# Product 7 of each projection in block products, with its shared terms added through an SBUF buffer

## The chip, the cores and the metric

The kernel runs on one core of a Trainium2 chip. The time is what the device takes for one execution of the whole program, in microseconds (us). Before the change it is 1493.05 us, the median of 10 runs that lie between 1492.59 and 1495.52 us.

## The reference

The input is x, 128 images of 128 nodes with 512 features each, and one 128x128 matrix adj with many zeros. Two layers follow each other, and both work on h, the layer norm of their input with negative values set to 0. All numbers are float32. Cut to what matters:

```python
h = jnp.maximum(_layernorm(x, axis=-1), 0.0)
A = jnp.einsum('od,bdn->bon', W1, h)            # W1 = W2 = adj
C = jnp.einsum('od,bdn->bon', W2, h) + b[None, :, None]
pre = A[:, :, None, :] + (C - A)[:, :, :, None]
x = x + jnp.max(jax.nn.relu(pre), axis=-1)      # layer 0

h = jnp.maximum(_layernorm(x, axis=-1), 0.0)    # layer 1
q = (h @ Wq + bq).reshape(b, n, H, HD)          # k and v the same; H, HD = 8, 64
scores = jnp.einsum('bihd,bjhd->bhij', q, k) / jnp.sqrt(jnp.float32(HD))
scores = scores + jnp.where(adj == 0, -1e9, 0.0)
out = jnp.einsum('bhij,bjhd->bihd', jax.nn.softmax(scores, axis=-1), v)
x = x + out.reshape(b, n, H * HD)
```

Layer 0 adds to each row of x one number per node, max(0, max over n of (adj @ h) + b), because A cancels on the diagonal of `pre`. A number that is the same for a whole row doesn't change a layer norm, so layer 1's h is that of layer 0, and the number (C in the kernel) is only added to x.

## The kernel before

The 128 images are worked on in 32 groups of G = 4. One pass of the main loop does, for group g: `apply(g - 1)` (attention weights times v, 128 small matmuls on TensorE, then reciprocals and products on VectorE), `scores(g)` (64 matmuls of q and k, and the exponentials on ScalarE), the projection v of group g, and the projections q and k of group g + 1. The norms of group g + 2, their adjacency products (adj @ h, one 128x512 matmul whose row maximum VectorE takes), the masks (GpSimd multiplies the exponentials by 0 or 1), the bias of v (`add_bv`), the number C (`add_c`, ScalarE) and the residuals of group g - 1 are spread over the pass.

The order in which each engine's instructions stand is written out by hand. Each projection is a list of six parts; v has parts 0 to 5, q 6 to 11, k 12 to 17. The table `todo` names what else is issued behind which part, and every engine works its own list from front to back.

A projection is a product of 512x512 matrices (512 rows of h, 512 outputs). It is computed after Strassen and Winograd: weights and activations are cut in quarters a11 to a22 and b11 to b22; sums s1 to s4 of the weight quarters (`weight_sum`) and t1 to t4 of the activation quarters (`h_sum`) are formed, and seven products of quarters replace eight. Products 1, 6 and 7 are accumulated in one another's terms, so that product 7's result stands in three outputs' sums: two of them take it, one through the term in `u3` (with product 5) and one through the PSUM bank of products 6 and 7, into which product 4 is accumulated afterwards.

Products 1, 6 and 7 are four matmuls each, 128x128 weights by 128x256 (`mm`, L453). Products 2, 3, 4 and 5 are split once more in the same way, into seven matmuls of 128x128 by 128x128 (`block_mm`, L561). The sums for that are `weight_blocks` (once, for the weights) and `h_blocks` (per group, on GpSimd, L380: one operation of 128x256 and two of 128x128 for each product). Three of the seven block products ("inner" ones) go straight into the PSUM bank of the product. The other four are shared by several outputs: they are accumulated in a scratch region (`run`, `five`) and added from there to the SBUF terms by VectorE (`more`, L579), step by step: the first and the fifth, then the sixth, then the seventh. Each next step accumulates into the same region, so it waits until VectorE has read the one before.

The terms lie in `pf` (product 1, with the terms of product 5's blocks) and in `u` (two parts, for the outputs that products 4 and 3 complete); `u` has two buffers. `add_pf` (L496, or L492 for v) adds a PSUM bank, a bias and `pf`. `add` (L474) writes an output as bank plus term. PSUM has eight banks, `bank(0)` to `bank(7)`, and a bank is used anew when its last reader is done.

Layout: h of a group is transposed by VectorE in blocks of 32 (`blocks`) and moved into place, `hT`, by 16 DMAs on SP's queue (`move`); `hT` has two buffers. All sums t1 to t4 and the results of `h_blocks` have one buffer each, so group g + 1's overwrite group g's.

In passes 0 and 31, v is computed with plain products. Product 7 is line `self.mm(self.b, "s3", "t3", ...)` in `p7`.

## Time and profile before

| what | value |
|---|---|
| median of 10 runs | 1493.05 us |
| the profiled execution | 1491.48 us |
| its span, first to last instruction | 1489.6 us |
| granted TensorE clock | 0.998 |
| TensorE busy (matmul) | 1472.1 us |
| VectorE / ScalarE / GpSimd busy | 1183.9 / 595.8 / 978.9 us |
| one pass of the loop (start of `apply` to the next, e.g. 773.65 to 819.32) | 45.67 us |

In the profile PE is TensorE, PEld its weight loads, DVE VectorE, ACT ScalarE, POOL GpSimd, and SP the engine that issues most DMAs. L453 is line 453 of the kernel. A line of a timeline gives the start, the time from the first start to the last end, the engine, the line, the operation, output <- inputs by name, and how often it stands there in a row; in brackets stands idle time before it and what ended it. The records of one TensorE instruction overlap with the next, so distances of starts tell its cost. A matmul of this kernel is two instructions.

### The profile page before, as it was taken

What the parts mean: (1) busy time and instruction counts of PE and PEld (TensorE: products, weight loads), DVE (VectorE), ACT (ScalarE), POOL (GpSimd) and SP (SyncE); (2) the same over time, 40 slices, a digit from 0 to 9 for tenths busy, and PEclk for the clock granted to TensorE, in tenths of its full rate; (3) what the DMA queues carried; (4) which work ended last, traced back from release to release, by engine and by line L of the source; (5) the groups of instructions that cost most, each with busy time, mean ns of one, the idle gap of its engine ahead of it and who ended that gap; (6) DMA issues with size and microseconds to landing.
All of it is one profiled execution on the core that took longest, in us unless ns stands there. A gap on an engine that the chain in (4) does not pass through costs nothing.

```text
span 1489.6 us, 36725 instructions
## 1 busy us (share of the span) xinstructions
PE 1472.1 (99%) x14013; PEld 1328.4 (89%) x14013; DVE 1183.9 (79%) x2869; ACT 595.8 (40%) x1179; POOL 978.9 (66%) x1238
## 2 busy tenths in 40 slices
PE   8999999999999999999999999999999999999997
PEld 6889989899998999898988999999999989899996
DVE  6787878878888878788787887788877878877886
ACT  3334343444344343434434443434434343444332
POOL 5887675667665676756677566766567675667660
PEclk9999999999999999999999999999999999999999
DMA  5221333212332223332123322233221233212211
GB/s 171 51 75 36 77 86 83 68 36 77 82 86 69 67 46 78 86 77 72 37 74 85 87 66 49 63 82 86 70 72 41 77 86 86 65 37 76 68 44 59
DMA packets 307826, 105.55 MB, mean 71 GB/s; under 512 B 273152, under 2 KB 273280, under 8 KB 307648
## 3 DMA queue, kind: packets, MB, share of 16 engines
q1 hardware_dynamic: 307328, 102.84, 27.6%
q8 instruction: 113, 1.85, 0.6%
q14 instruction: 65, 0.53, 0.1%
q0 software_dynamic: 176, 0.27, 0.1%
q10 hardware_dynamic: 144, 0.07, 0.0%
HBM read 37.03 MB, written 33.55 MB: 47 GB/s over the span
## 4 chain that ended last, share of the span: by engine, by line
PE 94%; POOL 2%; DVE 1%; DMA 1%; issue 0%; ACT 0%; SPq 0%; DVEq 0%; POOLq 0%
PE bk L561 39%; PE bk L453 33%; PE bk L720 8%; PE bk L690 8%; PE bk L343 7%; DMA wk_sb<-in_L_gnn_Wk_dram 1%; POOL ssq_sb L401 0%; POOL xp L311 0%; POOL o L750 0%; ACT hn L305 0%; DVE hs L367 0%; POOL rstd L286 0%; POOL h L380 0%; DVE ssk_sb L401 0%; POOL sq_sb L413 0%
## 5 line engine op out<-in xcount | busy, mean ns | idle before, releaser
L702 POOL TENSOR_TENSOR w<-w,live 128x512 f32<-128x512 f32 x248 | 309.2, 1274 | 0.0
L750 POOL TENSOR_TENSOR o<-xp,o 128x512 f32<-128x512 f32 x122 | 152.6, 1283 | 204.8 <-DVE o L738 174.9
L579 DVE TENSOR_TENSOR u<-u,bk 128x256 f32<-128x256 f32 x552 | 204.9, 412 | 57.7 <-PE bk L561 57.7
L698 ACT ACTIVATE w<-bk 128x512 f32<-128x512 f32 x256 | 128.8, 628 | 275.7 <-PE bk L690 275.7
L481 ACT COPY p1a<-bk 128x512 f32<-128x512 f32 x95 | 55.6, 586 | 388.7 <-PE bk L453 379.2
L380 POOL TENSOR_TENSOR h<-hT 128x256 f32<-128x256 f32 x93 | 68.2, 734 | 211.0 <-DMA hT<-tb 85.5
L579 DVE TENSOR_TENSOR p1a<-p1a,bk 128x128 f32<-128x128 f32 x368 | 109.4, 318 | 120.0 <-PE bk L561 62.9
L311 POOL TENSOR_TENSOR xp<-xp,bv_sb 128x512 f32<-128x512 f32 x128 | 160.1, 1271 | 32.3 <-ACT hn L305 32.3
L305 ACT ACTIVATE hn<-xp,nmr,rstd 128x512 f32<-128x512 f32 x124 | 100.9, 814 | 87.8 <-POOL nmr L288 47.9
L453 PE MATMUL bk<-hs,sk_sb 128*128 128x256 f32 x512 | 131.4, 380 | 0.0
L453 PE MATMUL bk<-sv_sb,hs 128*128 128x256 f32 x512 | 131.0, 380 | 0.0
L453 PE MATMUL bk<-hs,sq_sb 128*128 128x256 f32 x496 | 127.9, 380 | 0.0
L343 PE MATMUL bk<-hn,adjT 128*128 128x512 f32 x248 | 126.9, 593 | 0.0
L720 PE MATMUL bk<-v,w 128*64 128x65 f32 x4096 | 126.5, 222 | 0.0
L720 PEld LDWEIGHTS bk<-v,w 128*64 128x64 f32 x4096 | 122.1, 137 | 4.1 <-issue 0.3
L690 PE MATMUL bk<-qT,kT 64*128 64x128 f32 x2048 | 122.9, 275 | 0.0
L690 PEld LDWEIGHTS bk<-qT,kT 64*128 64x128 f32 x2048 | 116.8, 188 | 2.5 <-issue 0.3
L380 POOL TENSOR_TENSOR h<-hT,h 128x128 f32<-128x128 f32 x186 | 108.1, 581 | 14.6
L453 PEld LDWEIGHTS bk<-sv_sb,hs 128*128 128x128 f32 x512 | 90.4, 191 | 21.3 <-issue 14.3
L738 DVE TENSOR_TENSOR o<-bk,RS 128x448 f32<-128x448 f32 (+1 forms) x161 | 93.7, 582 | 7.2
L561 PEld LDWEIGHTS bk<-h,ssk_sb 128*128 128x128 f32 x558 | 81.8, 191 | 16.0 <-issue 14.3
L453 PEld LDWEIGHTS bk<-hs,sk_sb 128*128 128x128 f32 x512 | 87.8, 191 | 7.6 <-issue 0.7
(181 smaller groups left out, 3590.7 us busy)
## 6 DMA issues: line engine op xcount, KB each, us to landing
out_dram<-o SPq DMA_DIRECT2D x128, 256.0 KB, 2.6
xp<-in_x_dram SPq DMA_DIRECT2D x62, 512.0 KB, 4.0
hT<-tb SPq DMA_DIRECT2D x992, 32.0 KB, 1.9
xp<-in_x_dram SPq DMA_DIRECT2D x4, 256.0 KB, 4.3
wq_sb<-in_L_gnn_Wq_dram SPq DMA_DIRECT2D x2, 512.0 KB, 8.6
wk_sb<-in_L_gnn_Wk_dram SPq DMA_DIRECT2D x2, 512.0 KB, 10.9
wv_sb<-in_L_gnn_Wv_dram SPq DMA_DIRECT2D x2, 512.0 KB, 11.8
bv_sb<-in_L_gnn_bv_dram POOLq DMA_DIRECT2D x1, 256.0 KB, 8.0
```

What stands on the lines that cost most here:

```text
L305: nc.scalar.activation(HN[m], x_of(m), AF.Relu, scale=RSTD[m], bias=NMR[m])
L311: nc.gpsimd.tensor_tensor(x_m, x_m, bv_sb, op=ALU.add)
L343: nc.tensor.matmul(pa, adjT, HN[m], start=True, stop=True)
L380: nc.gpsimd.tensor_tensor(o, x, y, op=ALU.subtract)
L453: nc.tensor.matmul(bank[:, r, :], lhs, rhs, start=first and r == 0 and c == 0, stop=r == 1 and c == 1, skip_group_check=True,)
L561: nc.tensor.matmul(out, lhs, rhs, start=start, stop=True, skip_group_check=True)
L579: nc.vector.tensor_tensor(to, to, what, op=ALU.add)
L690: nc.tensor.matmul(psc[j][:, f, :], KT[g][r, f, i * D : (i + 1) * D], QT[g][r, f, i * D : (i + 1) * D], start=True, stop=True,)
L698: nc.scalar.activation(w[:, j], psc[j], AF.Exp, scale=HD ** -0.5)
L702: eng.tensor_tensor(w[:, j], w[:, j], live_h, op=ALU.mult)
L720: nc.tensor.matmul(pav[r, c : c + HE], w[:, h % 2, h // 2, r], V[:, i, h, :], start=True, stop=True,)
L750: eng.tensor_tensor(y, x_of(b), y, op=ALU.add)
```

## The change

Product 7 of q and k of groups 1 to 31, and of v in passes 1 to 30, is split into seven block products too. Its sums: a fifth set of weight blocks (`weight_blocks` of s3; for v in a tile of its own, for q and k in place of a quarter that is not needed) and a fifth `h_blocks` per group, of t3.

Its four shared block products are not added to one term but to two (product 7's result is in two outputs). So they are collected in a new SBUF buffer T7: ScalarE copies the first and the fifth into it, VectorE adds the sixth and the seventh, ScalarE copies the seventh into the one quarter that holds it alone. Then GpSimd adds the whole buffer, 128x512, to the two terms (`terms7(0)`, `terms7(1)`). `pf`, `u` and `u3` become one tile U of three parts with one buffer, and T7 has one buffer.

The order changes with it. The list of parts is now made by `steps`; product 5 of q, k and v has its first blocks ahead of product 6, product 7's first blocks stand between product 6's matmuls, and product 3's output (`end3`) is written in the second part of the next projection. The sums t3 and t4 (`h_sum` 0 and 3) go from VectorE to GpSimd. `h_blocks` is issued in its single operations, in another order. The adjacency product is split into `product` (TensorE) and `maximum` (VectorE). Norms, `blocks`, `move`, `add_bv` and masks are issued at other parts; the heads of `apply` are taken in the order 0, 2, 4, 6, 1, 3, 5, 7. The weight blocks of q and v in pass 0 are issued in other places and partly on VectorE instead of GpSimd.

The core of the diff (`u[:, 0]` is product 1's term and then product 7's, `u[:, 1]` goes to product 4's output, `u[:, 2]` to product 3's):

```diff
+    U = const.tile([P, 3, 2, N // 2], F32, name="u")
+    T7 = const.tile([P, 2, N // 2], F32, name="t7")
...
-        def h_blocks(g, k):
+        def h_blocks(g, k, parts=range(3)):
...
+            sums = (
                 (t[:, 0:2], b[:, :, 1], b[:, 0]),
                 (t[:, 2], b[:, 1, 1], t[:, 0]),
                 (t[:, 3], b[:, 1, 0], t[:, 2]),
-            ):
+            )
+            for i in parts:
+                o, x, y = sums[i]
                 nc.gpsimd.tensor_tensor(o, x, y, op=ALU.subtract)
...
+            def end7(self):
+                self.add_pf(self.u[:, 0], self.b, 1)
...
+            def end5(self):
+                self.add(self.dst(1, 1), self.c, self.u[:, 0])
...
+            def inner(self, k):
+
+                x = self.bk({5: self.c, 3: self.c, 7: self.b, 4: self.b, 2: self.a}[k])
+                a, b, s, t = self.parts_of(k)
+                self.block_mm(x[:, 0, 0], a[:, 0, 1], b[:, 1, 0])
+                self.block_mm(x[:, 0, 1], s[3], b[:, 1, 1])
+                self.block_mm(x[:, 1, 0], a[:, 1, 1], t[:, 3])
...
+            def sixth(self, k):
+                a, b, s, t = self.parts_of(k)
+                self.block_mm(self.run[k], s[2], t[:, 2])
+
+            def seventh(self, k):
+                a, b, s, t = self.parts_of(k)
+                self.block_mm(self.run[k], s[1], t[:, 1])
...
+            def first_to(self, k):
+                if k == 7:
+                    self.t = self.bk(T7)
+                    nc.scalar.copy(self.t[:, 0, 0], self.run[7])
+                    nc.scalar.copy(self.t[:, :, 1], self.five[7].unsqueeze(1).to_broadcast([P, 2, D]))
+                    return
+                self.add_blocks(k, 0, 0, 1)
...
+            def terms7(self, i):
+
+                u = self.u[:, i]
+                nc.gpsimd.tensor_tensor(u, u, T7, op=ALU.add)
+
+            def seventh_to(self, k):
+                if k == 7:
+                    nc.scalar.copy(self.t[:, 1, 0], self.run[7])
+                    self.add_blocks(7, 1, 1, 7)
+                    return
+                self.add_blocks(k, 1, slice(0, 2), 7)
+
+        def steps(p, tail, mid, t3):
+
+            t = tail + [lambda: None] * 8
+            return [
+                [t[0], p.p1],
+                [call(p.first, 5, True), call(p.first_to, 5), t[1], call(p.p6a, (0,)),
+                 call(p.first, 7, True), call(p.first_to, 7), call(p.p6a, (1, 2)),
+                 call(p.sixth, 5), call(p.sixth_to, 5), call(p.sixth, 7), call(p.sixth_to, 7),
+                 call(p.p6a, (3,)), call(p.seventh, 5), call(p.seventh_to, 5), p.end6],
+                [call(p.first, 2, True), call(p.seventh, 7), call(p.seventh_to, 7), call(p.terms7, 0), mid,
+                 call(p.inner, 2), p.end2, call(p.inner, 5), call(p.first43), call(p.first_to, 2),
+                 call(p.first_to, 4),
+                 call(p.inner, 7), t3, call(p.terms7, 1)],
+                [p.end7, p.end5],
+                [call(p.sixth, 2), call(p.sixth_to, 2), call(p.sixth, 4), call(p.sixth, 3), call(p.sixth_to, 4)],
+                [call(p.inner, 4), call(p.inner, 3), call(p.seventh, 2), call(p.seventh, 4),
+                 call(p.seventh, 3), call(p.seventh_to, 2), call(p.seventh_to, 4), p.end4],
+            ]
+
+        def later(p):
+            return [lambda: None, p.end3]
...
-                for h in range(H):
+                for h in (0, 2, 4, 6, 1, 3, 5, 7):
...
-                0: [(norm_end, m, False), (norm_end, m + 1, False)],
-                1: [(blocks, m)], 2: [(blocks, m + 1)],
-                4: [(adjacency, m)], 5: [(move, m + 1)], 7: [(adjacency, m + 1), (norm_act, m + 2)],
-                8: [(norm_end, m + 2), (add_bv, m), (add_bv, m + 1)],
-                13: [(norm_act, m + 3)], 14: [(norm_end, m + 3)], 16: [(adjacency, m + 2)],
+                1: [(norm_end, m, False)], 4: [(norm_end, m + 1, False)],
+                3: [(product, m)], 5: [(maximum, m)],
+                8: [(norm_act, m + 2)],
+                9: [(product, m + 1)], 10: [(blocks, m), (norm_end, m + 2, False), (norm_act, m + 3)], 11: [(blocks, m + 1), (move, m + 1), (maximum, m + 1)],
+                13: [(blocks, m + 2)], 14: [(norm_end, m + 3, False)],
+                15: [(product, m + 2)] + [(add_bv, m + i) for i in range(4)],
+                16: [(maximum, m + 2), (blocks, m + 3), (move, m + 3)],
...
+                    if p.n == "v":
+                        t3 = lambda: h_sum(g + 1, 0, nc.gpsimd)
+                    if p.n == "q":
+                        mid = lambda: [
+                            h_blocks(g + 1, k, (i,)) for k, i in ((0, 1), (1, 1), (0, 2), (1, 2))
+                        ]
...
-                        blocks(m - 2)
-                        blocks(m - 1)
-                        move(m - 1)
                         for i in range(G):
                             residual(b - G + i, nc.gpsimd)
...
+                    for k in (1, 2):
+                        add(4, h_sum, g + 1, k)
+                    for k, i in ((4, 0), (4, 1), (3, 0), (3, 1)):
+                        add(4, h_blocks, g + 1, k, (i,))
+                    add(5, h_sum, g + 1, 3, nc.gpsimd)
+                    for k, i in ((2, 0), (3, 2), (2, 1), (2, 2), (0, 0), (1, 0), (4, 2)):
+                        add(5, h_blocks, g + 1, k, (i,))
...
-                    for k, s in enumerate((8, 9, 9, 10, 10, 13, 14, 15)):
+                    for k, s in enumerate((8, 8, 9, 9, 14, 14, 14, 14)):
                         add(s, mask, nc.gpsimd, b + k // 2, k % 2)
...
-                    add(4, weight_blocks, nc.gpsimd, "v", (3, 2))
-                    add(15, weight_blocks, nc.gpsimd, "v", (0, 1))
+                    for s, k in ((0, 2), (0, 0), (1, 1)):
+                        add(s, weight_blocks, nc.vector, "q", (k,))
+                    for s, k in ((0, 3), (0, 2), (1, 0), (1, 1), (2, 4)):
+                        add(s, weight_blocks, nc.vector if k in (3, 2) else nc.gpsimd, "v", (k,))
+                    add(3, weight_blocks, nc.gpsimd, "q", (4,))
                     for i in range(G):
-                        add(15, add_bv, i)
+                        add((3, 3, 3, 11)[i], add_bv, i)
```

A part's own steps are issued first, then what `todo` names for it. `steps` is given for each projection; `tail` is `later` of the projection before, so its `end3` stands behind the first blocks of product 5.

## The prediction

> **What bounds the kernel now.** I read the page first (busy shares, then the chain that ended last), then one whole pass of the loop in the table by windows, then that pass in order of time, engine by engine.
>
> ```profile
> span 1489.6 us, 36725 instructions
> ...
> PE 1472.1 (99%) x14013; PEld 1328.4 (89%) x14013; DVE 1183.9 (79%) x2869; ACT 595.8 (40%) x1179; POOL 978.9 (66%) x1238
> ...
> PE 94%; POOL 2%; DVE 1%; DMA 1%; issue 0%; ACT 0%; SPq 0%; DVEq 0%; POOLq 0%
> ```
>
> ```profile
> core 0: us, PE busy (x) PEld busy (x) DVE busy (x) ACT busy (x) POOL busy (x), PEclk, DMA share, GB/s
> ...
> 773.65:819.32 45.67, 45.67 (x441) 41.41 (x441) 36.73 (x90) 18.69 (x37) 30.53 (x39) 1.00 0.28 70
> ```
>
> TensorE is the bound: 94% of the chain, no idle time in a pass, at a granted clock of 1.00. A pass (from the first matmul of `apply` to the next one) takes 45.67 us, and the others have room: VectorE 36.7, GpSimd 30.5, ScalarE 18.7 us. So less TensorE work shows in full as long as nobody makes TensorE wait.
>
> What one product costs is read from the starts of TensorE's instructions (two per matmul), not from their durations, which overlap:
>
> ```profile
> 786.39 0.38 PE L561 MATMUL bk<-wv_sb,h 128*128 128x128 f32 x2
> 786.61 0.39 PE L561 MATMUL bk<-wv_sb,hT 128*128 128x128 f32 x2
> ...
> 788.62 1.03 PE L453 MATMUL bk<-sv_sb,hs 128*128 128x256 f32 x4
> 789.49 0.38 PE L561 MATMUL bk<-ssv_sb,h 128*128 128x128 f32 x2
> 789.71 1.03 PE L453 MATMUL bk<-sv_sb,hs 128*128 128x256 f32 x4
> 790.58 0.38 PE L561 MATMUL bk<-sv_sb,hT 128*128 128x128 f32 x2
> ```
>
> Ten 128x128 blocks lie between 786.39 and 788.62: 0.223 us each. Product 7 is the four 128x256 matmuls from 788.62 to 790.58 with one block (789.49 to 789.71) between them: 1.96 - 0.22 = 1.74 us, 0.435 each.
>
> **The change, part by part.**
>
> *Product 7 in blocks.* Seven blocks for four matmuls: 7 x 0.223 = 1.56 against 1.74, a gain of 0.18 us. It applies to v in passes 1 to 30 and to q and k of groups 1 to 31, so 92 times: **-16.5 us**, and a pass of 45.67 - 0.54 = 45.13 us if nobody waits. The products' order around it moves the same matmuls, at no cost of their own.
>
> *GpSimd.* Its prices:
>
> ```profile
> 779.60 4.96 POOL L750 TENSOR_TENSOR o<-xp,o 128x512 f32<-128x512 f32 x4 [5.86 <-DVE o L738]
> ...
> 795.02 0.73 POOL L380 TENSOR_TENSOR h<-hT 128x256 f32<-128x256 f32 x1 [1.50 <-DVE hT L367]
> 795.83 1.32 POOL L380 TENSOR_TENSOR h<-hT,h 128x128 f32<-128x128 f32 x2
> 797.10 0.73 POOL L380 TENSOR_TENSOR h<-hT 128x256 f32<-128x256 f32 x1
> 797.91 1.43 POOL L380 TENSOR_TENSOR h<-hT,h 128x128 f32<-128x128 f32 x2
> 799.31 0.73 POOL L380 TENSOR_TENSOR h<-hs 128x256 f32<-128x256 f32 x1
> 800.11 0.99 POOL L380 TENSOR_TENSOR h<-hs,h 128x128 f32<-128x128 f32 x2
> ...
> 806.90 6.19 POOL L702 TENSOR_TENSOR w<-w,live 128x512 f32<-128x512 f32 x5
> ```
>
> Back to back, a 128x512 operation takes 1.23 us, a 128x256 one 0.73, a 128x128 one 0.46 (0.99 for two). A pass gets six adds of the buffer (`terms7`), two sums moved from VectorE (`h_sum` 0 and 3) and three operations of a fifth `h_blocks`: 8 x 1.23 + 0.73 + 2 x 0.46 = 11.5 us, so about 42 of 45.1. It still fits. What matters is where it is late.
>
> *The chain between v and q.* `h_sum` 0 overwrites a tile that v's product 7 reads until its third `inner` block, 17.2 us into the pass (scores end at 7.66, then v's matmuls at the prices above). From there GpSimd's queue holds, in order, without a pause: `h_sum` 0, `terms7(1)` of v, five first parts and six later parts of `h_blocks`, `h_sum` 3 among them, `terms7(0)` of q, four more later parts, `terms7(1)` of q. VectorE's `sixth_to(4)` of q stands behind that last add, since both add into u[:, 1], and TensorE's `seventh(4)` of q overwrites what `sixth_to(4)` reads; q's last blocks, k and the rest are queued behind it.
> GpSimd: 5 x 1.23 = 6.15; 5 first parts at 0.69, their 0.73 less the 0.04 by which independent neighbours overlap (1.27 lasts, 1.23 apart), = 3.45; 10 later parts, seven that follow something else at 0.41 and three that read the one before at 0.54 (795.83 and 800.11 rows: 0.46 and a gap of 0.08) = 4.49. Sum 14.1.
> To it comes contention: where a sum of two SBUF tiles runs on VectorE, the GpSimd operation that starts during it is stretched:
>
> ```profile
> 795.52 0.78 DVE L367 TENSOR_TENSOR hs<-hT 128x512 f32<-128x512 f32 x1
> ...
> 798.35 0.68 DVE L367 TENSOR_TENSOR hs<-hT,hs 128x512 f32<-128x512 f32 x1
> ```
>
> The pair at 795.83 takes 1.32 for 0.99, that at 797.91 1.43: 0.33 and 0.44 more. `h_sum` 1 and 2 stay on VectorE inside this chain: +0.77. The release of the tile costs 0.25 (the first L380 group of the pass starts that long after TensorE's slot ends), the add of `sixth_to(4)` and its hand-over 0.5 (L579, 0.41). Together 15.6 us.
> TensorE meanwhile has 45 blocks, 8 matmuls of 128x256 and 2 adjacency products (0.86 each): 10.04 + 3.46 + 1.72 = 15.2. So it waits **0.4 us in each of the 30 passes that have this chain, +11.7 us**. Bounds: 0 (no stretch, all parts overlapping: 13.7 + 0.75, earlier than needed) and 1.5 (all parts with gaps, 15.2, and both stretches). I take the middle sum because its rows are these very operations.
> The page "SBUF — State Buffer" of the Trainium skill (section "SBUF: two separate sides") says the pair of ports is an exclusive lock held for a whole instruction. By it the two sums would block 0.7 us each, 1.4 instead of 0.77, the wait 1.0 and the time 1508, an estimate from that page; the rows above show less than a whole instruction, so they decide here.
>
> *The hand-over on v alone.* `sixth_to(4)` of v waits for its `terms7(1)`, then `h_sum` 1 and 2 precede `seventh_to(4)`, which frees the bank that q's first blocks use. 17.45 + 2.5 + 0.35 (add) + 1.5 (the sums) + 0.17 (stretch) + 1.0 (three adds) = 23.0, needed at 22.8. This 0.2 lies inside the same 15.2 us and is not added.
>
> *end7.* From the end of `first43`, VectorE does three adds (0.33 apart, the 789.71 group of L579 is 1.05 for three) and the two halves of `end7` (L496, 0.88): 0.2 + 0.99 + 0.88 = 2.07 us; TensorE has `inner(7)`, an adjacency product and three sixths, 0.67 + 0.86 + 0.67 = 2.2, before it writes that bank. Nothing waits, with 0.1 us to spare; without the `product` there it would be 0.7 us late per product.
>
> *ScalarE and VectorE.* Three copies per product on ScalarE (0.24 by L263's 128x128 copy, up to 0.48 by L468 for the 128x256): +2.9 us a pass, under 22 of 45. VectorE gets 6 x 0.28 and loses 2 x 0.7. Both are covered by TensorE.
>
> *Masks and residuals.* k's `terms7(1)` waits for `first_to(4)`, 42.4 us in; four masks follow and end about 3.1 us into the next `apply`. The new order of heads needs the last one at 2.9 + 0.5 = 3.4. Covered with 0.3. Then come four `add_bv` (4.9), so the residuals start at 8 instead of 5.95, and norms end by 14.8; ScalarE's `norm_end(m)` stands ahead of v's last copy of the buffer, so `terms7(0)` of v starts at 15.5 and is needed by 17.7.
>
> *Moves.* SP issues 16 transfers in 11.2 to 11.4 us. Both moves now follow each other (from 35.7): 35.7 + 22.8 = 58.5, that is 13.4 into the next pass, landed (1.9) at 15.3, read at 17.4. The output stores wait behind them till 13.4; the residuals are only then written. Nothing is late.
>
> *Pass 0.* VectorE gets about 24 more `weight_blocks` operations there. Five groups at about 1.4 us (L401) now precede `end6` of v: from 47.2 to 54.2, +0.7, where TensorE needs it at 53.35: 1.6 us, and 0.9 more at the last product. Pass 1 lost 0.9 to late `add_bv` (46.57 against 45.67), and this goes: **+1.6 us**, between -1 and +4.
>
> Sum: -16.5 + 11.7 + 1.6 = **-3.2 us**. The profiled execution (1491.48 with 1.9 around its span) is 1.57 under the median of the runs; from the median 1493.05 I get 1489.9.
>
> **The rivals.**
> 1. *GpSimd is never late.* For it: the bound of 0; in 15.2 us a stretch of 0.4 decides. Against: both VectorE sums fall into the chain. Time: -16.5 + 1.6, to -16.5 + 6 + 1.6 with 0.2 us of waits: 1478 to 1484.
> 2. *Slower: the add into u[:, 1] on q comes later still.* Same place, `sixth_to(4)` of q behind `terms7(1)`, with gaps at every small operation. It decides from 0.5 us per pass on (16.5 - 1.6 = 14.9 over 30). At 0.9 us it costs 27: 1505; at 1.5, 1523. For it: GpSimd at 42 of 45 us and gaps of 0.08 us shown at dependent pairs. Against: most neighbours are independent.
> 3. *ScalarE holds k back.* `norm_end(m+2)` stands on its queue ahead of k's copies and waits for GpSimd's norms (1.05 us by L298 to L302) after q's last add; two norm passes (1.58) and k's first copies follow: 32.3 + 1.05 + 0.7 + 1.58 + 1.9 = 37.5, while k's `sixth(7)` would be at 37.4 to 37.8. Price 0.15 us per pass, +4.5: 1494.4.
> 4. *No saving on TensorE*, weight loads binding at 128 columns: excluded, 0.223 is measured with its loads.
>
> **How the numbers follow.** Forecast (waits of 0.2 to 0.55 us, 1484 to 1495) 0.34; rival 1, 0.22; rival 2, 0.34; rival 3, 0.10. The line at 0.2%, about 3 us, is what a measurement here tells from no change. Faster: all of rival 1 and 0.24 of the forecast, 0.46. Same: 0.08 of the forecast, 0.06 of rival 3, 0.02 of rival 2, 0.16. Slower: 0.38. Range: from rival 1's 1479 to waits of 1.05 us, 1493 + 31.5 - 14.9 = 1510, which leaves a tenth at each end.
>
> **What would show it.** A pass of 45.5 us with TensorE idle only before q's `seventh(4)`, near 32.4 us into it, and at q's first block; product 7 at 1.56 us; GpSimd near 42 us a pass; no idle in `apply` and none at `inner(4)`. It is wrong if TensorE waits at `inner(4)` for `end7`, or in `apply` for a mask, or if GpSimd's 20 operations take clearly under 14.5 or over 15.5 us.

## The result

The changed kernel takes 1503.29 us (median of 8 runs, 1501.84 to 1504.52) against 1493.23 us for the kernel before (28 runs): a ratio of 1.0067, interval [1.0059, 1.0076]. It is 10 us slower. The forecast was 1489.9 us with "faster" as the likeliest sign, and that sign was wrong. The time lies inside the range (1479 to 1510), but for other reasons than those on which the range's upper half was built.

From the page of the changed kernel (its profiled execution took 1502.45 us): the span, the busy times and the shares of the chain that ended last.

```profile
span 1500.7 us, 38618 instructions
...
PE 1474.8 (98%) x14565; PEld 1336.4 (89%) x14565; DVE 1224.0 (82%) x3016; ACT 653.0 (44%) x1455; POOL 1317.6 (88%) x1564
...
PE 93%; DVE 3%; issue 1%; POOL 1%; DMA 1%; ACT 0%; SPq 0%; DVEq 0%; POOLq 0%
```

TensorE is still the bound, but it is now idle for 25.9 us of the span instead of 17.5, and VectorE's share of the chain went from 1% to 3%. So one looks for places where TensorE waits for VectorE. The table by windows, with one row per pass of the loop, shows two of them (the columns are as in the prediction):

```profile
core 0: us, PE busy (x) PEld busy (x) DVE busy (x) ACT busy (x) POOL busy (x), PEclk, DMA share, GB/s
...
91.34:136.98 45.64, 45.60 (x460) 41.62 (x459) 37.36 (x95) 20.48 (x46) 41.59 (x50) 1.00 0.28 70
182.61:229.15 46.54, 45.85 (x459) 41.53 (x458) 38.57 (x95) 20.61 (x46) 41.60 (x50) 1.00 0.27 70
```

The normal pass of 45.64 us is as long as before (45.67), although product 7 costs less in each of the three projections. And some passes, like the second row, are 0.9 us longer, with VectorE 1.2 us busier. GpSimd is busy for 41.6 us of a pass, as forecast.

Where each microsecond went, from the starts of the first matmul of each `apply`, which mark the ends of the passes:

| stage | before | after | difference | in the prediction's sum |
|---|---|---|---|---|
| up to the first `apply` (the lead-in and pass 0) | 86.87 | 91.34 | +4.47 | +2.5 |
| pass 1 | 46.57 | 45.64 | -0.93 | -1.05 |
| passes 2 to 29, as if all were median ones (45.67, 45.655) | 1278.76 | 1278.34 | -0.42 | -4.2 |
| passes 2 to 29, what the longer ones have above that | 0.84 | 7.79 | +6.95 | 0 |
| pass 30 | 43.24 | 45.64 | +2.40 | -0.15 |
| from the start of pass 31 to the last instruction | 33.32 | 31.95 | -1.37 | 0 |
| span | 1489.6 | 1500.7 | +11.1 | |

(The last column splits the prediction's terms by stage: 0.54 us gained and 0.39 us waited in each pass from 1 to 30, 2.5 us lost in pass 0 and 0.9 us won back in pass 1. The remainder to its -3.2 us is the two products of group 1 in pass 0. Each column is one execution. Two kernels further down that differ only in pass 30 reach the first `apply` at 90.62 and 91.54, so the first row is known to about 1 us.)

**The normal pass.** TensorE's starts show the gain of product 7 at the size that was forecast. The distance between starts is at least 0.110 us for one instruction of a 128x128 block and 0.215 us for one of a 128x256 matmul, in both kernels. A pass before has 168 and 72 of these, a pass after 210 and 48: 42 x 0.110 - 24 x 0.215 = -0.54 us. But the distances above these minima sum to 0.61 us in a pass before and to 1.12 us in a pass after: +0.51 us. In the fastest kernel further down (a pass of 45.31 us) 0.33 us of these are gone, and 0.18 us stay as gaps of 0.03 to 0.06 us. About 0.33 us of the 0.51 lies in one place, at q's first blocks. There TensorE starts its blocks with gaps, as the timelines of TensorE and VectorE show for the pass that began at 91.34:

```profile
113.86 0.43 PE L587 MATMUL bk<-h,wq_sb 128*128 128x128 f32 x2
114.34 0.46 PE L587 MATMUL bk<-hT,sq_sb 128*128 128x128 f32 x2
114.63 0.60 PE L481 MATMUL bk<-hs,sq_sb 128*128 128x256 f32 x2
```

```profile
111.47 0.83 DVE L379 TENSOR_TENSOR hT<-hT 128x512 f32<-128x512 f32 x1
112.34 0.83 DVE L379 TENSOR_TENSOR hs<-hT 128x512 f32<-128x512 f32 x1
113.09 0.41 DVE L639 TENSOR_TENSOR v<-v,bk 128x256 f32<-128x256 f32 x1
113.42 0.74 DVE L665 TENSOR_TENSOR u<-u,bk 128x256 f32<-128x256 f32 x2
```

The block (two instructions) at 113.86 takes 0.48 us from start to start and the next one 0.29, where a block takes 0.22 elsewhere. VectorE's two sums (`h_sum` 1 and 2, L379) stand ahead of v's last adds (L639, L665), which read the bank that q's first blocks overwrite. This is the "hand-over on v alone" of the prediction.

The chain on GpSimd behind it is there too, with the lengths that the prediction worked out. These are its rows from `h_sum` 0 to the middle, and its last add:

```profile
108.57 1.27 POOL L379 TENSOR_TENSOR hs<-hT 128x512 f32<-128x512 f32 x1 [0.67 <-PE bk L587]
...
111.83 0.79 POOL L396 TENSOR_TENSOR h<-hs,h 128x128 f32<-128x128 f32 x1
112.58 1.17 POOL L396 TENSOR_TENSOR h<-hT 128x256 f32<-128x256 f32 x1
...
122.22 1.26 POOL L690 TENSOR_TENSOR u<-u,t 128x512 f32<-128x512 f32 x1
```

From 108.57 to 123.48 are 14.9 us (forecast 14.1 + 0.77), and the two operations that meet VectorE's sums are stretched by 0.33 and 0.44 us over their 0.46 and 0.73. But TensorE doesn't wait for the last add, because it has already lost the time at q's first blocks.

**The long passes.** The timeline of VectorE in a normal pass (first fence) and in a long one (second), about 11 us into the pass:

```profile
147.52 0.69 DVE L352 TENSOR_REDUCE amax<-bk 128x1 f32<-128x512 f32 x1 [2.46 <-PE bk L348]
148.25 0.54 DVE L354 TENSOR_SCALAR c<-amax,b_sb 128x4 f32<-128x4 f32 x1
148.71 0.47 DVE L639 TENSOR_TENSOR u<-u,bk 128x128 f32<-128x128 f32 x2
```

```profile
193.16 0.69 DVE L352 TENSOR_REDUCE amax<-bk 128x1 f32<-128x512 f32 x1 [2.45 <-PE bk L348]
193.88 1.80 DVE L354 TENSOR_SCALAR c<-amax,b_sb 128x4 f32<-128x4 f32 x1
195.59 0.47 DVE L639 TENSOR_TENSOR u<-u,bk 128x128 f32<-128x128 f32 x2
```

The operation at L354 adds a bias to four numbers per partition and clips them: the number C. It took 0.23 us in passes 2 to 29 before. It now takes 0.52 to 0.55 us in 21 of the passes 1 to 29, and 1.80 us in the other 8, which are the long ones. The adds at L639 that free the region for v's sixth block stand behind it on VectorE. TensorE then waits for them:

```profile
195.92 0.49 PE L587 MATMUL bk<-wv_sb,h 128*128 128x128 f32 x2 [0.62 <-DVE u L639]
```

GpSimd runs the four residuals of the group before at that time, back to back (1.23 us apart), in both passes:

```profile
145.03 4.95 POOL L816 TENSOR_TENSOR o<-xp,o 128x512 f32<-128x512 f32 x4
...
190.67 4.95 POOL L816 TENSOR_TENSOR o<-xp,o 128x512 f32<-128x512 f32 x4
```

The short C operation ends at 148.79, just behind the boundary between the third residual and the fourth (145.03 + 3 x 1.23 = 148.7); the long one, which starts the same 0.47 us ahead of that boundary, misses it and ends at 195.68, behind the end of the fourth (195.6). In each of the passes 1 to 29 it ends 0.03 to 0.07 us behind the end of a residual. So this tiny operation waits for a gap between GpSimd's operations, and it sometimes loses the first gap.

The kernel before shows the same effect in its pass 1. There late `add_bv` operations had made the residuals late, and C, which starts 11.72 us into every pass, fell beside the last of them:

```profile
94.75 4.95 POOL L750 TENSOR_TENSOR o<-xp,o 128x512 f32<-128x512 f32 x4
```

```profile
98.59 1.13 DVE L346 TENSOR_SCALAR c<-amax,b_sb 128x4 f32<-128x4 f32 x1
```

It ended at 99.72, behind the residuals' end at 99.70, and TensorE's next block of v came 0.35 us late (99.97). The price of C beside a residual stood in the trace of the kernel before.

**Pass 0.** VectorE's adds stand behind the weight operations that were moved to it. TensorE waits for 2.1 us at 52.3, 1.55 us at 62.3 and 0.9 us at 69.6. The chain of VectorE at the first of these, and TensorE:

```profile
53.34 0.54 DVE L422 TENSOR_TENSOR ssv_sb<-wv_sb,ssv_sb 128x128 f32<-128x128 f32 x1
53.81 0.68 DVE L517 TENSOR_TENSOR u<-bk,u 128x512 f32<-128x512 f32 x1
```

```profile
54.63 2.33 PE L481 MATMUL bk<-sv_sb,hs 128*128 128x256 f32 x5 [1.96 <-DVE u L517]
```

A weight operation like these takes 0.28 us where GpSimd is idle (55.12). Where it is not, most take longer: 0.54 us (53.34) or 1.35 us (58.68).

**Pass 30** has one adjacency product instead of four. Before, it was 2.4 us shorter than the other passes for that reason. Now the 2.6 us of the missing three (0.86 each) are spent on waits instead:

```profile
1440.98 0.71 PE L587 MATMUL bk<-ssv_sb,h 128*128 128x128 f32 x4 [0.28 <-DVE u L665]
...
1453.58 0.68 PE L587 MATMUL bk<-h,ssq_sb 128*128 128x128 f32 x4 [0.38 <-DVE u L665]
```

These are the sixth blocks, which wait for VectorE's three adds of the first ones (L665, 1439.85 to 1440.93).

### The profile page after: what moved, and what is told of

Read it like the earlier page. It is cut to its first block, busy times and chain, and to the rows that moved or that the text cites. A ratio compares the mean times of both kernels' runs of the same rounds, so it can differ in the third digit from the quotient of the medians.

```text
span 1500.7 us, 38618 instructions
## 1 busy us (share of the span) xinstructions
PE 1474.8 (98%) x14565; PEld 1336.4 (89%) x14565; DVE 1224.0 (82%) x3016; ACT 653.0 (44%) x1455; POOL 1317.6 (88%) x1564
## 4 chain that ended last, share of the span: by engine, by line
PE 93%; DVE 3%; issue 1%; POOL 1%; DMA 1%; ACT 0%; SPq 0%; DVEq 0%; POOLq 0%
PE bk L587 48%; PE bk L481 22%; PE bk L786 8%; PE bk L756 8%; PE bk L348 7%; PE bk L732 1%; DMA xp<-in_x_dram 1%; DVE amax L352 0%; DVE ssk_sb L422 0%; POOL w L768 0%; POOL xp L314 0%; POOL o L816 0%; DVE ssq_sb L422 0%; PE bk L340 0%; DVE u L639 0%
## 5 line engine op out<-in xcount | busy, mean ns | idle before, releaser
L690 POOL TENSOR_TENSOR u<-u,t 128x512 f32<-128x512 f32 x184 | 234.3, 1273 | 86.0 <-DVE t L639 62.2
L665 DVE TENSOR_TENSOR u<-u,bk 128x256 f32<-128x256 f32 x552 | 206.6, 415 | 43.8 <-PE bk L587 26.6
L639 DVE TENSOR_TENSOR u<-u,bk 128x128 f32<-128x128 f32 x368 | 109.0, 316 | 79.6 <-PE bk L587 78.7
L352 DVE TENSOR_REDUCE amax<-bk 128x1 f32<-128x512 f32 x128 | 86.7, 677 | 74.7 <-PE bk L348 74.7
L508 ACT COPY u<-bk 128x512 f32<-128x512 f32 x95 | 55.0, 579 | 183.5 <-PE bk L481 175.7
L587 PE MATMUL bk<-ssv_sb,h 128*128 128x128 f32 x720 | 111.6, 277 | 0.3 <-DVE u L665 0.3
L587 PEld LDWEIGHTS bk<-ssv_sb,h 128*128 128x128 f32 x720 | 98.5, 191 | 14.5 <-issue 13.9
L812 ACT ACTIVATE xp<-xp,c 128x512 f32<-128x512 f32 x128 | 91.2, 715 | 5.3 <-POOL xp L314 5.3
L321 DVE STREAM_TRANSPOSE tb<-hn 128x512 f32<-128x512 f32 x124 | 87.0, 702 | 2.4 <-ACT hn L308 2.4
L587 PEld LDWEIGHTS bk<-h,ssq_sb 128*128 128x128 f32 x558 | 74.7, 192 | 14.9 <-issue 7.2
L396 POOL TENSOR_TENSOR h<-hT,h 128x128 f32<-128x128 f32 x186 | 83.6, 457 | 4.9
```

Source lines behind the costliest of these rows:

```text
L587: nc.tensor.matmul(out, lhs, rhs, start=start, stop=True, skip_group_check=True)
L639: nc.vector.tensor_tensor(to, to, what.to_broadcast(to.shape), op=ALU.add)
L665: nc.vector.tensor_tensor(to, to, what, op=ALU.add)
L690: nc.gpsimd.tensor_tensor(u, u, T7, op=ALU.add)
```

## The experiments

Two theories stood against each other for the long passes: **(A)** the C operation waits for GpSimd's residuals, because both read and write only SBUF, and **(B)** the adds at L639 are late for another reason and C only stands there. For the normal pass: the hand-over at q's first blocks, or GpSimd's chain behind it. All ratios are against the kernel before on the same chip.

### C on ScalarE

```diff
-                nc.vector.tensor_scalar(C[g], AMAX[g], b0_sb, 0.0, op0=ALU.add, op1=ALU.max)
+                nc.scalar.activation(C[g], AMAX[g], AF.Relu, bias=b0_sb)
```

> Only C = max(0, amax + b0) of a group moves from VectorE to ScalarE; everything else is the changed kernel. Theory A (the port): in ten passes this 128x4 operation takes 1.80 us on VectorE instead of 0.54, because it finds no gap between GpSimd's residuals, and the first blocks' adds of v queue behind it; TensorE then stands 0.78 us before v's sixth block. Then all passes should be 45.64 us, none 46.5, and the time should fall by 10 x 0.88 = 8.8 us, to 1494.5 (1493 to 1496). Rival B (late norms or a late load of x, which the chain that ended last also shows): the long passes stay, 1503 +- 1.5.

Measured: 1495.76 us, ratio 1.0022 [1.0013, 1.0031], so by the two ratios 6.7 us faster than the changed kernel. (The expectation counted ten long passes; the trace has eight.) Of the 30 passes 28 are 45.63 to 45.68 us, one is 45.8 and one 46.03 (the changed kernel has a pass of 46.03 too, with a longer gap at q's first blocks; what makes it is not known). ScalarE does it in 0.30 us beside the same residuals:

```profile
149.13 0.30 ACT L354 ACTIVATE c<-amax,b_sb 128x4 f32<-128x4 f32 x1 [0.51 <-DVE amax L352]
...
145.92 4.96 POOL L816 TENSOR_TENSOR o<-xp,o 128x512 f32<-128x512 f32 x4
```

Theory A holds: it is VectorE's C operation beside the residuals. (ScalarE's reads and writes only SBUF too and isn't held up, so that alone is not the reason.) The two kernels further down in which the residuals end before C starts agree with it: there the operation takes 0.23 us in each of the passes 1 to 29, still on VectorE.

### One sum behind the hand-over

```diff
+                    if p.n == "v":
+                        part[5].insert(7, lambda: h_sum(g + 1, 2))
...
-                    for k in (1, 2):
+                    for k in (1, 2) if g == 0 else (1,):
                         add(4, h_sum, g + 1, k)
...
+                    for k, i in ((2, 0), (3, 2)):
+                        add(5, h_blocks, g + 1, k, (i,))
                     add(5, h_sum, g + 1, 3, nc.gpsimd)
-                    for k, i in ((2, 0), (3, 2), (2, 1), (2, 2), (0, 0), (1, 0), (4, 2)):
+                    for k, i in ((2, 1), (2, 2), (0, 0), (1, 0), (4, 2)):
```

> The second sum on VectorE (h_sum 2) goes behind v's seventh_to(4), so that the bank that q's first blocks use is free earlier; on GpSimd two operations of h_blocks go ahead of h_sum 3, which needs that sum. Theory C (the hand-over on v is what holds TensorE): the 0.33 us before q's first blocks go in 29 passes, -9.6 us, to about 1494. Theory D (the step of the prediction: GpSimd's chain of 20 operations up to the last add of q holds TensorE): the wait moves to q's seventh(4), at about 32.5 us into the pass, and the time stays within 2 us of 1503.

Measured: 1495.08 us, ratio 1.0021 [1.0012, 1.0030]. The normal pass is 45.52 us, 0.13 less. The gap at q's first blocks is gone, and a smaller one stands where the prediction had put the wait, 32.6 us into the pass. VectorE's timeline there:

```profile
1083.38 0.42 DVE L665 TENSOR_TENSOR u<-u,bk 128x256 f32<-128x256 f32 x1 [0.41 <-POOL u L690]
```

So both waits are real and lie one behind the other: who takes the first away gains 0.13 us and then meets the second. Only 4 passes were long instead of 8, which gives 3.5 us of the gain. The edit doesn't touch C or the residuals, so I put that down to the changing luck of C at the boundary. The runs of this kernel spread over 4.4 us (1493.66 to 1498.10), those of the kernel with both repairs over 2.0, which fits, but no run settles it.

### Without GpSimd's adds of the buffer

```diff
             def terms7(self, i):
...
-                nc.gpsimd.tensor_tensor(u, u, T7, op=ALU.add)
+                return
```

The kernel leaves the six adds of a pass out, so the terms of product 7's shared blocks are missing in two outputs.

> The six adds per pass of the buffer on GpSimd are left out (the terms of product 7's shared blocks are then missing in both outputs); the blocks, the copies and VectorE's adds stay. Theory D: GpSimd's chain is 3.7 us shorter, TensorE waits nowhere between v and q, and as GpSimd is 7.4 us per pass lighter its residuals end before C is due, so the long passes go too: 45.2 us a pass, 1503 - 13 - 9 = 1481 (1478 to 1486). Theory C alone: the adds matter only in that sixth_to(4) of v starts 0.4 us earlier, 1490 to 1494.

Measured: 1484.78 us, ratio 0.9949 [0.9933, 0.9964]. The pass is 45.26 us and none is long: without 7.6 us of GpSimd's work the residuals stand earlier and end before C starts.

```profile
147.80 0.23 DVE L354 TENSOR_SCALAR c<-amax,b_sb 128x4 f32<-128x4 f32 x1
```

```profile
142.69 4.96 POOL L816 TENSOR_TENSOR o<-xp,o 128x512 f32<-128x512 f32 x4 [4.67 <-DVE o L804]
```

45.26 is 0.13 above the 45.13 that the prediction gave for a pass in which nobody waits. But pass 0 (91.27 to the first `apply`) and pass 30 (45.42) stay as they are, so they don't come from the adds of the buffer.

### Product 7 as four matmuls, in the new order

```diff
-                 call(p.first, 7, True), call(p.first_to, 7), call(p.p6a, (1, 2)),
-                 call(p.sixth, 5), call(p.sixth_to, 5), call(p.sixth, 7), call(p.sixth_to, 7),
+                 call(p.p6a, (1, 2)),
+                 call(p.sixth, 5), call(p.sixth_to, 5),
...
-                [call(p.first, 2, True), call(p.seventh, 7), call(p.seventh_to, 7), call(p.terms7, 0), mid,
+                [call(p.first, 2, True), mid,
...
-                 call(p.inner, 7), t3, call(p.terms7, 1)],
+                 lambda: p.mm(p.b, "s3", "t3"), t3],
...
-                    for k, i in ((4, 0), (4, 1), (3, 0), (3, 1)):
+                    for k, i in ((3, 0), (3, 1)):
```

> Product 7 is again four matmuls of 128x256, without buffer, adds and the fifth h_blocks; all else of the change stays: the new order of norms, masks, moves, sums and weight blocks. It measures the order alone. If the blocks give their 0.18 us each and the order is free, this takes 45.67 us a pass and 1493 + 4.5 (pass 0) = 1497. If the new order itself costs (theory E: the sums on GpSimd, the late residuals), it is slower than 1500; if the order is what makes room, passes are 45.4 to 45.7 and the time 1490 to 1497.

Measured: 1511.07 us, ratio 1.0124 [1.0109, 1.0140]. The expectation had "slower than 1500" for the case that the order itself costs, but not with this cause. The pass is 46.22 us, 0.55 above the kernel before, the residuals start 5.9 us into the pass and are not late, and C takes 0.23 us in the passes 1 to 29. TensorE stops for some 0.1 us twice in each projection, at 12.5, 25.0 and 37.5 us into the pass. In TensorE's timeline, for v:

```profile
520.34 0.60 PE L481 MATMUL bk<-sv_sb,hs 128*128 128x256 f32 x2
520.88 0.49 PE L587 MATMUL bk<-wv_sb,h 128*128 128x128 f32 x2
521.21 0.39 PE L587 MATMUL bk<-wv_sb,hT 128*128 128x128 f32 x2
```

520.34 to 520.88 is 0.54 us for two matmul instructions that need 0.43. VectorE's add of the first blocks (L639) runs from 520.54 to 520.83, just ahead of the block at 520.88. The new order needs product 7's blocks: they lie between the steps of product 5 and hide VectorE's adds there. So within this order the blocks are worth 0.58 us a pass, and the order without them costs as much.

### Both repairs

C on ScalarE and the late sum together (the two diffs above).

> C on ScalarE and h_sum 2 behind v's seventh_to(4), both at once. Theories A and D together: no pass of 46.4 us (A), all at 45.51 (D: the hand-over's 0.33 us is gone, 0.1 comes back at q's seventh(4)). 30 x 0.13 = 3.9 us under the kernel with C alone on ScalarE: 1492 (1490.5 to 1493.5). If the two were the same wait seen twice, it would stay at 1495.

Measured: 1491.73 us, ratio 0.9992 [0.9983, 1.0001], as expected. The pass is 45.54 us. The change as made, with these two edits, would have been no measurable difference.

### Pass 30: product 7's inner blocks earlier

On top of both repairs, in pass 30 alone (`early` is true there):

```diff
-                 call(p.inner, 2), p.end2, call(p.inner, 5), call(p.first43), call(p.first_to, 2),
-                 call(p.first_to, 4),
-                 call(p.inner, 7), t3, call(p.terms7, 1)],
-                [p.end7, p.end5],
+                 call(p.inner, 2), p.end2] + ([call(p.inner, 7), p.end7] if early else []) + [
+                 call(p.inner, 5), call(p.first43), call(p.first_to, 2), call(p.first_to, 4)] + (
+                 [] if early else [call(p.inner, 7)]) + [t3, call(p.terms7, 1)],
+                [p.end5] if early else [p.end7, p.end5],
```

> As before, and in pass 30 alone inner(7) and end7 stand ahead of inner(5) and the first blocks of products 4 and 3. Theory F: pass 30 takes as long as the others, although it has no adjacency products, because nothing lies between inner(7) and inner(4) there and TensorE waits 0.5 to 0.7 us for end7 in each of v, q and k; then pass 30 falls from 45.4 to about 43.2 us and the time by 2.2 us, to 1490 (1489 to 1491). Rival: it waits for the order of GpSimd or for the masks, and pass 30 stays within 0.5 us.

Measured: 1493.94 us, ratio 1.0007 [0.9998, 1.0016]: 2.2 us slower than without the edit, not faster. Pass 30 went from 45.44 to 47.77 us. I had read its waits as waits for `end7`. TensorE's timeline with the edit shows that they are not:

```profile
1429.83 0.49 PE L587 MATMUL bk<-ssv_sb,h 128*128 128x128 f32 x2 [0.29 <-DVE v L639]
1430.82 0.71 PE L587 MATMUL bk<-ssv_sb,h 128*128 128x128 f32 x4 [0.51 <-DVE u L665]
```

The sixth blocks wait for the adds of the first ones (L639, L665), and the three inner blocks of product 7 were the work that still lay between the two once the adjacency product was missing. The edit took this cover away too.

### Pass 0: the weight operations ahead of the loop

On top of the last kernel, the four older sets of q's weight blocks are made by GpSimd ahead of the loop and two of v's sets by VectorE between the plain products of k:

```diff
-                2: [(adjacency, G + 1)], 3: [(blocks, G + 3), (move, G + 3)],
-                4: [(adjacency, G + 2)], 5: [(adjacency, G + 3)],
+                2: [(adjacency, G + 1)], 3: [(blocks, G + 3), (move, G + 3), (weight_blocks, (nc.vector, "v", (3,)))],
+                4: [(adjacency, G + 2), (weight_blocks, (nc.vector, "v", (2,)))], 5: [(adjacency, G + 3)],
...
-            weight_blocks(nc.gpsimd, "q", (3,))
+            weight_blocks(nc.gpsimd, "q", (3, 2, 0, 1))
...
-                    for s, k in ((0, 2), (0, 0), (1, 1)):
-                        add(s, weight_blocks, nc.vector, "q", (k,))
-                    for s, k in ((0, 3), (0, 2), (1, 0), (1, 1), (2, 4)):
-                        add(s, weight_blocks, nc.vector if k in (3, 2) else nc.gpsimd, "v", (k,))
+                    for s, k in ((1, 0), (1, 1), (2, 4)):
+                        add(s, weight_blocks, nc.gpsimd, "v", (k,))
```

> As before, and the weight blocks of q are formed on GpSimd ahead of the loop and two sets of v on VectorE ahead of it, so that in pass 0 VectorE has one set per part. Theory G: of the 4.5 us that the first apply starts later, the sets ahead of end6 and end5 of v are the cause (stalls of 2.1 and 1.55 us on TensorE, and the lower clock after the first); the first apply starts at 87 to 88.5 instead of 91 to 92 us and the time is 1486.5 (1485 to 1489). Rival: the sets on GpSimd hold h_blocks back instead, and the first apply stays later than 90.

Measured: 1496.91 us, ratio 1.0028 [1.0016, 1.0039], a miss: the first `apply` comes at 93.81 instead of 91.54. VectorE's weight operations now stand beside GpSimd's sums of q's weights, and TensorE waits 3.5 us for the row maximum behind them. VectorE's and GpSimd's timelines:

```profile
40.48 1.31 DVE L422 TENSOR_TENSOR wv_sb<-wv_sb,sv_sb 128x128 f32<-128x128 f32 x1
41.71 1.34 DVE L422 TENSOR_TENSOR wv_sb<-sv_sb 128x128 f32<-128x128 f32 x1
42.98 1.35 DVE L422 TENSOR_TENSOR wv_sb<-sv_sb,wv_sb 128x128 f32<-128x128 f32 x1
```

```profile
41.60 1.31 POOL L434 TENSOR_TENSOR sq_sb<-wq_sb 128x512 f32<-128x512 f32 x1
42.87 1.31 POOL L434 TENSOR_TENSOR sq_sb<-wq_sb,sq_sb 128x512 f32<-128x512 f32 x1
```

An operation of 0.28 us takes 1.31 to 1.35, as long as the GpSimd operation beside it: the two engines take turns, one operation each. It is the same effect as with C, and here it comes with every operation.

### The chain shortened: q's second add on the finished output

On top of both repairs, q's second add of the buffer leaves the chain: GpSimd adds T7 to the finished output behind `end4`, a norm moves by one part, and two masks by two.

```diff
+        def late7(p):
+            d = p.dst(1, 0)
+            nc.gpsimd.tensor_tensor(d, d, T7, op=ALU.add)
...
-                 call(p.inner, 7), t3, call(p.terms7, 1)],
+                 call(p.inner, 7), t3] + ([] if p.n == "q" else [call(p.terms7, 1)]),
...
-                 call(p.seventh, 3), call(p.seventh_to, 2), call(p.seventh_to, 4), p.end4],
+                 call(p.seventh, 3), call(p.seventh_to, 2), call(p.seventh_to, 4), p.end4] + (
+                    [call(late7, p)] if p.n == "q" else []),
...
-                9: [(product, m + 1)], 10: [(blocks, m), (norm_end, m + 2, False), (norm_act, m + 3)], 11: [(blocks, m + 1), (move, m + 1), (maximum, m + 1)],
+                9: [(product, m + 1)], 10: [(blocks, m), (norm_end, m + 2, False)], 11: [(norm_act, m + 3), (blocks, m + 1), (move, m + 1), (maximum, m + 1)],
...
-                    for k, s in enumerate((8, 8, 9, 9, 14, 14, 14, 14)):
+                    for k, s in enumerate((8, 8, 11, 11, 14, 14, 14, 14)):
```

> On the kernel with C on ScalarE and h_sum 2 late: q's second add of the buffer goes to the finished output, behind end4 of q, and out of the chain that sixth_to(4) of q waits for; two masks and a norm stand behind it now. Theory D: the chain between v and q is 1.23 us shorter, so the last wait there (0.1 us at q's seventh(4), 0.1 at k's first blocks) goes: 45.51 becomes 45.25 to 45.35 us a pass, 5 to 8 us less, 1484 to 1487. Rival: GpSimd's add is only late elsewhere (k's copies into the buffer wait for it), passes of 45.5 or more, 1492 to 1500.

Measured: 1483.90 us, ratio 0.9940 [0.9927, 0.9954]: 9 us faster than the kernel before, and the lowest time of all the kernels here. In the table by windows a pass now has no idle TensorE:

```profile
499.72:545.03 45.31, 45.31 (x459) 41.63 (x458) 36.62 (x94) 21.01 (x47) 41.63 (x50) 1.00 0.29 71
```

45.31 us is the same pass as without the adds of the buffer (45.26), give or take 0.05. So the adds are all but hidden once nothing queues behind q's last one. GpSimd is as busy as before the edit (41.6 us): what cost the 0.23 us was not its load as such, but who stood behind it and when. Of the 0.23 us, 0.13 were at q's seventh block and 0.09 at k's first ones; the norm and the masks moved too, and no run separates their part.

### Pass 0 again: q's weights on GpSimd

On top of the last kernel:

```diff
-            weight_blocks(nc.gpsimd, "q", (3,))
+            weight_blocks(nc.gpsimd, "q", (3, 2, 0, 1))
...
-                    for s, k in ((0, 2), (0, 0), (1, 1)):
-                        add(s, weight_blocks, nc.vector, "q", (k,))
```

> Edit against e8: the block products' weights of q are all made by GpSimd ahead of the loop, as in the kernel before, so VectorE loses 12 of the 28 weight operations that stood in pass 0 between the end of the plain products of k and the last add of v. Theory (VectorE is the bound from 46 to 70 us of pass 0, and TensorE's stalls of 2.3 and 1.55 us there are waits for adds queued behind those operations): VectorE is some 5 us less busy there, the 2.3 us stall goes, the first apply comes 2 to 4 us earlier than in e8 (91.9), the time is 1480 to 1482. Rival (GpSimd becomes the bound of pass 0, as when the weights of v were made by VectorE beside GpSimd's weight sums, e7): the norms of groups 1 and the first h_blocks come 5 us later, the stall only moves, first apply at 91 to 94, time 1483 to 1486. Passes 1 to 29 stay at 45.3 us by both.

Measured: 1485.55 us, ratio 0.9957 [0.9943, 0.9970]; the first `apply` comes at 92.73 (91.92 without the edit). The rival's numbers came in. The first `apply` is known to about 1 us, so the edit gained nothing, and whether it cost anything isn't shown. The stall at v's adds is gone, and TensorE waits for GpSimd's first `h_blocks` instead. From the table of TensorE's waits of this kernel (us in total, times, the longest):

```profile
PE bk L587 <- POOL h L396: 5.0, 2, 4.7
```

Between 46 and 66 us of this pass VectorE is busy for 18.9 and GpSimd for 19.2 of the 20 us (19.2 and 15.3 without the edit), so moving work from one to the other only moved the wait. In the kernel before, VectorE was busy for 15.6 of the same 20 us, and in the changed one for 19.5: the change adds 12 operations for the new weight blocks and puts some older ones on VectorE. TensorE's waits stand behind these, but no run made pass 0 as short as before, so that this is the whole reason isn't shown.

## Why the prediction was wrong, step by step

- **"Product 7 in blocks": right.** 0.54 us less matmul time in each pass, by the starts of both kernels; -16.2 us for the 30 passes. The last kernel but one keeps 0.36 us of it per pass; 0.18 us go to small gaps of 0.03 to 0.06 us that every kernel with these blocks has.
- **"The chain between v and q": length right, place wrong, size nearly right.** 14.9 us of GpSimd were forecast and measured, with the stretches of 0.33 and 0.44 us. The wait was forecast at 0.39 us at q's seventh block. The time beyond the minima grew by 0.51 us; 0.33 of it are waits that the experiments took away, and they stood at q's first blocks.
- **"The hand-over on v alone … lies inside the same 15.2 us and is not added": right as arithmetic, but it comes first.** TensorE loses the time there, and the chain then has it to spare. The experiment with the late sum showed the second wait right behind the first.
- **"Masks and residuals": this is the step that failed.** The prediction moved the residuals to 8 us and asked only whether they would be late. It didn't ask which VectorE operations they would now stand beside. It named the end of the norms at 14.8 and v's copy, and left out the C operation at 11.3 us and the adds behind it. This term stood at nothing in the sum and cost 7.0 us net, nearly all of it in 8 passes; with C on ScalarE it was gone. The 0.9 us that pass 1 of the kernel before lost were read as the price of late `add_bv` alone, though C, blocked for 1.13 us there, made about half of them (0.46 us at v's blocks).
- **The rule that was set aside.** The prediction weighed the Trainium skill's page "SBUF — State Buffer" (section "SBUF: two separate sides"), an exclusive lock for a whole instruction, against two rows that showed less, and took the rows. For those two operations the rows were right again (0.33 and 0.44 us). For the weight operations and for C the trace agrees with the page: 1.31 to 1.35 us for 0.28, and C waits for the end of a GpSimd operation, in 8 passes even of a second one (1.80 for 0.23). The mistake was to read a price from one pair of operations, where GpSimd's were the short ones and waited for VectorE, and to use it also where VectorE's is short and waits for GpSimd's 1.23 us.
- **"Pass 0": +2.5 forecast, +4.5 measured.** The add of v ended at 54.5, as worked out (54.2 and 0.7), but TensorE needed it at 52.3 and not at 53.35, since a stall of 1.1 us at 31.5 of the kernel before had gone. The weight operations beside GpSimd at 1.35 us made the next add late, too (1.55 us). The gain in pass 1 (-0.93, forecast -1.05) was right.
- **"end7: without the `product` there it would be 0.7 us late per product": said, and not put into the sum.** Pass 30 is the pass without it: +2.4 us. The wait is not at `end7`, as this step had it, but at the sixth blocks, as the experiment on pass 30 showed.
- **Rival 2** (slower, a later add into u[:, 1]) had the right sign for another reason: the add was never the last to arrive. **Rival 3** (ScalarE holds k back) did not happen; a wait of 0.09 us at 37.3 us, near its place, appears only once q's first blocks are in time, and is gone in the kernel that moves the norm.

By the prediction's own terms: -16.2 for the blocks, +15.3 beyond the minima in the passes (0.51 x 30; 11.7 of waits forecast), +7.0 for C, +2.4 for the last pass, +3.5 for passes 0 and 1 together (1.6 forecast) and -1.4 at the end give +10.6, against +11.1 in the span. The forecast of -3.2 is 14.3 us from that: 7.0 are C, 3.6 the passes' gaps, 2.4 pass 30 and 1.9 passes 0 and 1, less 1.4 at the end; 0.8 us are left unassigned.

What stays open: why C wins the first gap in 21 passes and loses it in 8, although it starts 0.44 to 0.49 us ahead of GpSimd's boundary in both kinds; and pass 22, which begins near 1045 us and takes 45.9 to 46.0 us in four of these kernels.

## What to carry to other kernels

When an operation is moved, list what runs beside it on the other engine at its new place, not only whether it is in time: a four-element operation of VectorE on SBUF beside a run of GpSimd operations can cost a whole one of them, and everything queued behind it. A fix can be tiny: the same operation on ScalarE, at 0.30 us. And a pass without its usual filler (the first, the last) has to be summed by itself, because each wait that the filler hides shows there.

## What the runs showed of the hardware

- A VectorE `tensor_scalar` of 128x4, all in SBUF, takes 0.23 us alone, 0.54 us or 1.80 us beside GpSimd operations of 1.23 us that run without a pause, and ends 0.03 to 0.07 us behind the end of one of them.
- A VectorE sum of 128x128 takes 0.28 us beside an idle GpSimd, mostly 0.43 to 0.58 beside GpSimd operations of 128x128, and 1.31 to 1.35 beside those of 128x512.
- The granted clock of TensorE fell to 0.54 behind the wait in pass 0, although the wait was only 2.1 us long. In the changed kernel's table by windows (the wait, then the 3.7 us behind it):

```profile
52.30:54.50 2.20, 0.38 (x2) 0.00 (x0) 2.17 (x6) 1.79 (x3) 2.12 (x5) 1.00 0.76 183
54.50:58.20 3.70, 3.57 (x9) 2.89 (x10) 3.60 (x11) 0.12 (x1) 2.01 (x4) 0.54 0.46 176
```

With both repairs the wait at the same place was 2.3 us and the clock stayed at 1.00, so the length of the wait alone doesn't decide it. It cost little: the slow matmuls filled time in which that kernel waited for VectorE instead (1.67 us at 58.9), and its first `apply` came only 0.7 us earlier.
